# The output projection's seventh block product, split into quarter products

## The chip, the cores and the metric

The kernel runs on one core of one Trainium2 chip. The metric is the device time of one execution in microseconds (us). The core's engines are TensorE (matmuls; "PE" in the profile, with "PEld" for its weight loads), VectorE ("DVE"), ScalarE ("ACT"), GpSimd ("POOL") and SyncE ("SP"), which here issues all DMAs. Each engine takes its own instructions strictly in the order in which the program wrote them, and waits for other engines at semaphores.

## The reference

Two attention layers, one after the other, over eight images of 512 channels and 32 x 32 = 1024 positions, in float32. Cut to what matters, for one layer and with `w` and `b` as its weights:

```python
xn  = group_norm(x) * gn_scale + gn_bias          # 8 groups in layer 0, 32 in layer 1
qkv = einsum('oc,bcn->bon', qkv_w, xn) + qkv_b
q, k, v = split into 8 heads of 64 channels
att = softmax(einsum('bhdi,bhdj->bhij', q, k) / 8, axis=-1)
out = einsum('bhij,bhdj->bhdi', att, v)           # back to 512 channels
x   = einsum('oc,bcn->bon', proj_w, out) + proj_b + x
```

The change concerns the last line, the output projection with its residual `x`: a product of a 512 x 512 matrix with a 512 x 1024 matrix, a bias for each row, and the old `x` added.

## The kernel before, in words

The work is cut into sixteen units, one for each image of each layer. Pass u of the main loop (u from 0 to 15) runs the projections to q, k and v of unit u (`projections`), then the output projection of the unit before it, u − 1 (`project`), and then the attention of unit u (`attention`). So fifteen output projections run in this way, in passes 1 to 15; the last unit's runs after the loop (`project_last`). Below, "pass 5" means the pass of unit 5, with the output projection of unit 4 in it. Layer 0 is units 0 to 7, layer 1 units 8 to 15. The order on every engine is the order in which these Python functions are called; there is no scheduler (`manual_schedule`).

A product of two large matrices is not formed directly. `blocks` cuts both factors into 2 x 2 blocks and forms seven block products in place of eight (Winograd's variant of Strassen's method), with sums and differences of the blocks made beforehand on VectorE and GpSimd. The left factors are sums of weight blocks (`mix_weights`), the right ones sums of data blocks (`mix_right`, whose four parts are called `mixing`). The seven products are formed in the order 1, 6, 2, 7, 5, 4, 3. They accumulate in three pairs of PSUM banks, which `blocks` calls `bx`, `by` and `bz`; they are the same as `apair[0]` (called `x` in the plans), `sbank[0]` and `apair[1]` (called `z`). A fourth pair, `sbank[1]`, is called `s1`. Products 1 and 2 use `bx`, products 6, 7 and 4 accumulate one after the other in `by`, products 5 and 3 in `bz`. Between them VectorE takes sums out of `by`: after product 6 `u2 = by + p1`, after product 7 `u3 = by + p1`, where `p1` is the copy of product 1 that ScalarE made. A result block is named by its row half r and its column half h: (0, 0) comes after product 2, (1, 1) after product 5 as `bz + u3`, (1, 0) after product 4 as `by + p1`, (0, 1) after product 3 as `bz + u2`. `done` is called after each of the seven, with a count g.

A block product may itself be formed in quarters: `inner_products` cuts its 2 x 2 factor blocks once more and forms seven small products of 128 x 128 by 128 x 256 in place of four matmuls of 128 x 128 by 128 x 512. Four of these small products (1, 6, 7 and 5 of the inner order) don't go to the block's own bank: 1, 6 and 7 accumulate in a region `one`, 5 goes into a region `two`, and after each of the four ScalarE copies the region to an SBUF tile of the rest (`m2`, `m4` and so on, "m_o" in the profile). GpSimd then adds two quarters of the rest together (`fold`, L468 and L469) and adds the rest to every result block that the product belongs to (`rests`). An entry of `plan` gives the inner product's `one`, `two`, order and room. Which block products are formed in quarters stands in `INNER`; in the output projection ("o") it is products 2, 3 and 4.

An inner product wants its own left and right factors. The right ones ("ro" in the profile) are made in `mix_o` by four VectorE subtractions of 128 x 256, and the left ones ("lo") were made once for each layer by GpSimd or VectorE (`mix_inner_left`), stored in DRAM, and are loaded in each pass; in pass 9, the first to use those of layer 1, they are made on the spot by GpSimd (`make_left`). All of this is hung into the projections of the next unit by the dictionary `parts`: `parts[g]` runs after the g-th block product of the q, k and v projections, of which 15 to 21 belong to v.

What is particular to passes 7 and 9: in pass 7 GpSimd and VectorE also make the inner left factors of q and k for layer 1 (`made_parts`, ten parts of four operations), some in the projection at g = 3, the others on VectorE at fixed steps of the attention (`left_parts`), and VectorE mixes weights of layer 1. In pass 9 it is the output projection's turn.

In `project`, `done` adds the bias and `x` (the tiles `w.res`) to `u2`, `u3` and `p1` by pairs of L703; `others` adds PSUM to these sums (L737); `rests` adds a rest and stores the result (L745, `store`).

The attention of a unit has eight chunks of eight steps. In each step TensorE forms scores (L820), ScalarE their exponentials (L828), VectorE sums these (L865, L867) and TensorE multiplies by v (L848). Its first scores need the bank that `others(1, 0)` has just emptied, and its third those of `others(0, 1)`.

Of the kernel before, what the change touches and what calls it, by code (L numbers as in the profile page):

```python
# [18 lines left out]
P = 128  # L19
# [13 lines left out]
def fast_path(ctx, tc, x, qkv_wT, proj_wT, vecs, groups, out, flag):  # L33
# [24 lines left out]
    BL = 32  # L58
    SCALE = 1.0 / math.sqrt(D)

    INNER = {"q": (2, 5, 4, 3), "k": (1, 2, 7, 5, 4, 3), "o": (2, 3, 4)}
    assert D == H and C == FD

    def pool(name, bufs, **kw):
# [477 lines left out]
    def room_of(pool, tag):  # L542
        return lambda name: pool.tile([P, 2, FD], F32, tag=tag, name=name)
# [151 lines left out]
    def project(w, after):  # L695


        l, b = units[w.u]
        dst = mid[b] if l == 0 else out[b]
        g = 0  # L700

        def plus(to, o, cols, more):
            return nc.vector.scalar_tensor_tensor(  # L703
                to, cols, vec[:, l, PB, o : o + 1], more, ALU.add, ALU.add
            )

        def done(sums):

            nonlocal g
            g += 1  # L710
            for i in range(2):
                if g == 2:
                    u2 = sums[1][:, i, :]
                    plus(u2, i, w.res[i][:, FD:], u2)
                elif g == 4:
                    u3 = sums[2][:, i, :]
                    plus(u3, 2 + i, w.res[2 + i][:, FD:], u3)
                elif g == 5:
                    p1 = sums[0][:, i, :]
                    plus(p1, 2 + i, w.res[2 + i][:, :FD], p1)  # L720
            after(g)

        results = {}

        def store(o, h):
            nc.sync.dma_start(dst[o * P : (o + 1) * P, ts(h, FD)], results[o, h])

        def c11(bank, *_):
            for i in range(2):
                cols = results[i, 0] = w.res[i][:, :FD]  # L730
                plus(cols, i, bank[:, i, :], cols)

        def others(r, h, bank, more, _=None):
            for i in range(2):
                o = 2 * r + i
                results[o, h] = more[:, i, :]
                w.evac[h] = nc.vector.tensor_add(more[:, i, :], bank[:, i, :], more[:, i, :])  # L737
                if (r, h) == (1, 1):
                    store(o, h)

        def rests(r, h, rest, _):
            for i in range(2):
                o = 2 * r + i
                cols = results[o, h]
                nc.gpsimd.tensor_add(cols, cols, rest[:, i, :])  # L745
                store(o, h)

        w.evac = [None, None]
        x, z, s1 = apair[0], apair[1], sbank[1]
        tmp = room_of(tmppool, "tmp")  # L750
        plan = {
            2: (s1, z, ORDER, tmp), 4: (x, s1, ORDER, tmp), 3: (s1, x, ORDER, room_of(accpool, "acc"))
        }
        inner = {k: (*w.inner_o[k], *plan[k]) for k in w.inner_o}
        w.taken = blocks(
            f"o_{w.u}", w.left, w.right_o, False, c11, others, done, (rbpool, "rb"), plain_sum, inner, rests
        )

# [26 lines left out]
    def attention(w, at_step, at_end):  # L785
# [189 lines left out]
        def bias_last():  # L975
# [4 lines left out]

        parts = {
            3: [lambda: reciprocals(CC - 1)], 10: [lambda: divide(CC - 1)], 14: [bias_last],
            17: mixing[:2], 21: [mixing[3], mixing[2]],
        }

        w.inner_o = {}
# [14 lines left out]
        def make_left(i):  # L1001
            w.making[i](lefts[3 * i : 3 * i + 3], later=behind_loads)

        def mix_o(k):
            tag = {2: "x2", 3: "x1", 4: "x4"}[k]
            room = tpool.tile([P, 4, FD2], F32, tag=tag, name=f"ro{k}_{u}")
            if k == INNER["o"][-1]:
                w.inner_o[k] = mix_inner_in(w.right_o[k], room, nc.vector)
                lefts.append(room[:, 3, :P])
                if u == B:  # L1010
                    make_left(2)
                else:
                    nc.sync.dma_start(lefts[-1], src[:, len(lefts) - 1, :])
            else:
                w.inner_o[k], subs = mix_inner(w.right_o[k], room, nc.vector)
                for part in subs:
                    part()
# [3 lines left out]
                w.inner_o[k] = (inner_lefts(k, w.left[k], lefts[3 * i : 3 * i + 3]), w.inner_o[k])  # L1021

        parts[15] = [load_left]
        if u == B:
            parts[20] = [partial(make_left, 0), partial(make_left, 1)]
        parts[18] = [partial(mix_o, 2)]
        parts[21] += [partial(mix_o, 4), partial(mix_o, 3)]
        w.finish = finish
        return parts

# [36 lines left out]
    for u in range(2 * B):  # L1067
# [84 lines left out]
        if old is not None:  # L1152
# [4 lines left out]
            def after(g):  # L1157
                stats_of(*stats_after.get(g, ()))
                if u == B - 1:
                    for part, room in zip(made_parts[:3], rooms) if g == 3 else ():  # L1160
                        part(room)

            project(old, after)
            if u == B - 1:
                left_v, mixing_w = mix_weights(1, load_weights(1, (2,)), nc.vector, 2)
                lefts = lefts + left_v
                left_parts = {
                    (c, 3 if c else 6): partial(made_later, c, part)
                    for c, part in enumerate(made_parts[3:])
                }  # L1170
            w.evac_before, w.taken_before = old.evac, old.taken
            if u == B:
# [313 lines left out]
```

## Time and profile before

| what | us |
|---|---|
| median of 8 runs | 3258.44 |
| lowest and highest of the runs | 3258.10, 3259.56 |
| the profiled execution, by its own time | 3258.73 |
| its span, first to last instruction | 3256.9 |
| granted TensorE clock | 1.000 of full speed |
| an attention (pass 5, 893.15 to 1003.41) | 110.26 |
| projections to q, k and v (pass 5, 801.83 to 870.26) | 68.43 |
| the output projection (pass 5, 870.26 to 893.15) | 22.89 |

The time of an execution is the span and some 1.8 us around it. A row of the timeline has a start, a length, the engine, the line of the code, the operation, the tile that is written and those that are read, and the number of like instructions merged into it; in brackets is the time for which the engine stood idle before it, and who ended that. Tile names leave buffer numbers out: `s` is one of the two `sbank`s, `a` one of the `apair`s. Busy times of the engines in three projections and in the first chunk of an attention, from the view by stretches:

```profile
core 0: us, PE busy (x) PEld busy (x) DVE busy (x) ACT busy (x) POOL busy (x), PEclk, DMA share, GB/s
870.26:893.15 22.89, 22.89 (x76) 13.85 (x74) 20.77 (x32) 5.12 (x12) 7.07 (x8) 1.00 0.53 205
1475.02:1497.91 22.89, 22.89 (x76) 13.85 (x74) 22.21 (x33) 5.11 (x12) 13.21 (x20) 1.00 0.64 240
1879.98:1902.87 22.89, 22.89 (x75) 13.85 (x73) 22.49 (x32) 5.11 (x12) 14.61 (x18) 1.00 0.61 209
893.15:906.90 13.75, 13.75 (x129) 5.00 (x132) 11.82 (x11) 8.36 (x9) 5.66 (x5) 1.00 0.21 79
```

The first row is pass 5, an ordinary one; the second is pass 7 and the third pass 9.

### The profile page before, as it was taken

To read this page: it belongs to the slowest core of one execution; us is meant where nothing else is said; L and a number is where in the kernel's file an instruction comes from. 1 tells how busy PE (TensorE), PEld (TensorE's weight loads), DVE (VectorE), ACT (ScalarE), POOL (GpSimd) and SP (SyncE) were. 2 spreads that over 40 slices of the span, in tenths; PEclk is the share of its full clock that TensorE was granted. 3 is DMA by queue.
4 is the path that set the end of the run, shared out by engine and by line. 5 is a ranking of instruction groups with operands and counts; after the bars stand their busy time and mean duration, and the time that the engine had idled before them with its cause. 6 is when DMAs were issued, how large, how long until landed. Compare 5 with 4: busy or idle time off the path is not lost.

```text
span 3256.9 us, 56805 instructions
## 1 busy us (share of the span) xinstructions
PE 3244.3 (100%) x22206; PEld 1863.4 (57%) x22206; DVE 2714.5 (83%) x3488; ACT 1650.8 (51%) x2296; POOL 1215.3 (37%) x1207
## 2 busy tenths in 40 slices
PE   9999999999999999999999999999999999999999
PEld 5465474654746547465574655747556474564743
DVE  5887978789787897989979889797897978979786
ACT  1653627546274463744637446373563735537354
POOL 2054171531706317063270732607126071350710
PEclk9999999999999999999999999999999999999999
DMA  3112120121201212023120121201212012120111
GB/s 104 48 45 79 46 79 28 45 79 46 85 22 45 85 44 85 18 71 114 55 86 27 45 86 46 86 15 45 86 46 85 17 49 81 46 85 22 68 70 48
DMA packets 86464, 192.51 MB, mean 59 GB/s; under 512 B 22961, under 2 KB 34993, under 8 KB 84273
## 3 DMA queue, kind: packets, MB, share of 16 engines
q1 hardware_dynamic: 86192, 188.82, 16.9%
q8 instruction: 180, 2.95, 0.4%
q14 instruction: 92, 0.75, 0.1%
HBM read 148.00 MB, written 39.19 MB: 57 GB/s over the span
## 4 chain that ended last, share of the span: by engine, by line
PE 96%; DVE 3%; issue 0%; DMA 0%; ACT 0%; SPq 0%; DVEq 0%
PE a L848 26%; PE s L820 25%; PE s L416 14%; PE a L416 12%; PE a L455 10%; PE s L455 9%; DVE acc L867 1%; PE a L820 1%; PE s L766 0%; PE a L766 0%; DVE tr L880 0%; PE s L361 0%; DVE acc L865 0%; DVE ao L874 0%; DMA xn<-x_dram 0%
## 5 line engine op out<-in xcount | busy, mean ns | idle before, releaser
L828 ACT ACTIVATE p<-s 128x1024 f32<-128x1024 f32 x976 | 998.5, 1025 | 557.8 <-PE s L820 514.9
L848 PE MATMUL a<-p,v 64*64 64x512 f32 x8192 | 1099.9, 589 | 0.0
L820 PE MATMUL s<-q,k 64*64 64x512 f32 x7808 | 1058.2, 590 | 0.0
L867 DVE TENSOR_TENSOR acc<-acc,p 128x1024 f32<-128x1024 f32 x768 | 967.9, 1260 | 61.5 <-ACT p L828 12.8
L848 PEld LDWEIGHTS a<-p,v 64*64 64x64 f32 x8192 | 383.3, 131 | 495.8 <-ACT p L828 350.3
L820 PEld LDWEIGHTS s<-q,k 64*64 64x64 f32 x7808 | 383.6, 133 | 431.8 <-issue 422.6
L1088 POOL TENSOR_TENSOR r<-xn 128x256 f32<-128x256 f32 x30 | 49.5, 1649 | 1175.8 <-DVE acc L867 1038.3
L650 POOL TENSOR_TENSOR k<-k,m_k 128x512 f32<-128x512 f32 x180 | 259.5, 1462 | 0.0
L865 DVE TENSOR_TENSOR acc<-p,p 128x1024 f32<-128x1024 f32 x128 | 156.6, 1224 | 21.7 <-ACT p L828 13.9
L312 POOL TENSOR_TENSOR y<-var,half 128x4 f32<-128x4 f32 (+1 forms) x17 | 33.2, 1951 | 344.2 <-DVE var L310 344.2
L880 DVE STREAM_TRANSPOSE tr<-acc 128x1024 f32<-128x1024 f32 x128 | 158.0, 1234 | 0.0
L650 POOL TENSOR_TENSOR q<-q,m_q 128x512 f32<-128x512 f32 x120 | 157.2, 1325 | 0.0
L890 DVE TENSOR_REDUCE red<-tr 128x32 f32<-128x1024 f32 x128 | 154.4, 1207 | 0.6
L538 DVE TENSOR_TENSOR u_v<-s,p_v 128x1024 f32<-128x1024 f32 x32 | 39.2, 1224 | 123.8 <-PE s L416 123.8
L501 ACT COPY p_o<-a 128x1024 f32<-128x1024 f32 x15 | 15.2, 1013 | 244.2 <-PE a L416 244.2
L874 DVE TENSOR_TENSOR ao<-a,tmp 128x512 f32<-128x512 f32 x128 | 88.1, 688 | 60.9 <-ACT tmp L873 59.8
L460 ACT COPY m_q<-s 128x256 f32<-128x256 f32 x150 | 55.9, 373 | 145.3 <-PE s L455 142.8
L468 POOL TENSOR_TENSOR m_o<-m_o 128x256 f32<-128x256 f32 x45 | 34.3, 762 | 251.5 <-ACT m_o L460 251.5
L416 PE MATMUL s<-x_t,s2w 128*128 128x512 f32 x256 | 117.5, 592 | 0.0
L416 PE MATMUL a<-w,xn 128*128 128x256 f32 x496 | 112.1, 379 | 0.0
L460 ACT COPY m_k<-s 128x256 f32<-128x256 f32 x165 | 61.5, 373 | 93.7 <-PE s L455 90.2
L334 ACT ACTIVATE xn<-xn,shift,scale 128x512 f32<-128x512 f32 x124 | 99.6, 805 | 10.8 <-DVE shift L330 10.8
(291 smaller groups left out, 5129.1 us busy)
## 6 DMA issues: line engine op xcount, KB each, us to landing
rb<-drec SPq DMA_DIRECT2D x128, 256.0 KB, 3.9
xn<-mid SPq DMA_DIRECT2D x36, 512.0 KB, 7.6
il<-ilk SPq DMA_DIRECT2D x15, 1152.0 KB, 6.7
xn<-x_dram SPq DMA_DIRECT2D x32, 512.0 KB, 7.2
x<-x_dram SPq DMA_DIRECT2D x32, 512.0 KB, 5.4
x<-mid SPq DMA_DIRECT2D x28, 512.0 KB, 4.7
il<-ilq SPq DMA_DIRECT2D x15, 768.0 KB, 4.2
mid<-u_o SPq DMA_DIRECT2D x32, 256.0 KB, 2.0
```

Source lines behind the costliest of these rows:

```text
L334: nc.scalar.activation(cols, cols, AF.Identity, bias=st["shift"][:, c - lo : c - lo + 1], scale=st["scale"][:, c - lo : c - lo + 1],)
L416: nc.tensor.matmul(dst, at[:, c, ts(i, P)], moving[:, c, :], start=start and c == 0 and not (tokens and i % 2), stop=stop and c == 1, skip ...
L455: nc.tensor.matmul(dst[j], a[j], b[j], start=j in (1, 5) or first and j in (2, 4), stop=j not in (1, 6), skip_group_check=True,)
L460: taken.append(nc.scalar.copy(to[j], dst[j]))
L650: w.last[sel].append(add(cols, cols, rest[:, i, :]))
L820: nc.tensor.matmul(bank[e * H : (e + 1) * H, j, :], w.k[pr][j * H : (j + 1) * H, t * P + e * H : t * P + (e + 1) * H], w.q[pr][j * H : (j ...
L828: exp = nc.scalar.activation(p, bank, AF.Exp, scale=SCALE)
L848: nc.tensor.matmul(banks[r][j * H : (j + 1) * H, :], w.v[rows, t, lo : lo + D], p[rows, j, :], start=(t == 0), stop=(t == NT - 1),)
L865: nc.vector.tensor_add(acc, state["first"], p)
L867: nc.vector.tensor_add(acc, acc, p)
L880: nc.vector.transpose(tr, state["acc"].pop(c))
L890: nc.vector.tensor_reduce(red[:, :, qh, :], state["tr"].rearrange("p j (f i) -> p j f i", i=BL), AX.X, ALU.add)
```

## The change

The seventh block product of the output projection is formed in quarters too. For that it gets right factors (`mix_o(7)`, in a tile of `accpool`, made one block product earlier than those of 4 and 3, together with the difference that it needs, `mixing[3]`), left factors (two of them in that tile, two in the tile of product 4), regions (`s1` and `z`; product 2 now takes `z` and `s1` in place of `s1` and `z`) and a room for its rest (tile "o2"; the rest of product 3 moves from `accpool` to "o1"). Its rest is added to two result blocks: (1, 1), which is now stored after that addition and not straight after `others`, and (1, 0), which is stored after the second of its two additions. The bias and `x` are added to `p1` at g = 4 and no longer at g = 5. In passes 0 and 9 there are four parts of left factors to be made and not three. In pass 7 two parts of those of q and k, not three, are made by GpSimd in the projection, and VectorE makes one more in the attention, at step 6 of its second chunk.

```diff
-    INNER = {"q": (2, 5, 4, 3), "k": (1, 2, 7, 5, 4, 3), "o": (2, 3, 4)}
+    INNER = {"q": (2, 5, 4, 3), "k": (1, 2, 7, 5, 4, 3), "o": (2, 3, 7, 4)}
...
-                elif g == 5:
+            for i in range(2):
+                if g == 4:
                     p1 = sums[0][:, i, :]
                     plus(p1, 2 + i, w.res[2 + i][:, :FD], p1)
...
-                if (r, h) == (1, 1):
-                    store(o, h)
-
-        def rests(r, h, rest, _):
+
+
+        to_come = [(1, 0)]
+
+        def rests(r, h, rest, _=None):
             for i in range(2):
                 o = 2 * r + i
                 cols = results[o, h]
                 nc.gpsimd.tensor_add(cols, cols, rest[:, i, :])
-                store(o, h)
+                if (r, h) not in to_come:
+                    store(o, h)
+            if (r, h) in to_come:
+                to_come.remove((r, h))
...
-            2: (s1, z, ORDER, tmp), 4: (x, s1, ORDER, tmp), 3: (s1, x, ORDER, room_of(accpool, "acc"))
+            2: (z, s1, ORDER, tmp), 7: (s1, z, ORDER, room_of(tpool, "o2")),
+            4: (x, s1, ORDER, tmp), 3: (s1, x, ORDER, room_of(tpool, "o1")),
...
-            17: mixing[:2], 21: [mixing[3], mixing[2]],
+            17: mixing[:2], 20: [mixing[3]], 21: [mixing[2]],
...
-            tag = {2: "x2", 3: "x1", 4: "x4"}[k]
-            room = tpool.tile([P, 4, FD2], F32, tag=tag, name=f"ro{k}_{u}")
-            if k == INNER["o"][-1]:
+            pool, tag = {2: (tpool, "x2"), 7: (accpool, "acc"), 3: (tpool, "x1"), 4: (tpool, "x4")}[k]
+            room = pool.tile([P, 4, FD2], F32, tag=tag, name=f"ro{k}_{u}")
+            if k in (7, 4):
                 w.inner_o[k] = mix_inner_in(w.right_o[k], room, nc.vector)
-                lefts.append(room[:, 3, :P])
-                if u == B:
-                    make_left(2)
-                else:
-                    nc.sync.dma_start(lefts[-1], src[:, len(lefts) - 1, :])
+                n = len(lefts)
+                lefts.extend(room[:, 3, i * P : (i + 1) * P] for i in range(2))
+                if u != B:
+                    nc.sync.dma_start(
+                        room[:, 3, :].rearrange("p (s o) -> p s o", s=2), src[:, n : n + 2, :]
+                    )
...
         parts[15] = [load_left]
+        parts[18] = [partial(mix_o, 2)]
+        parts[20].append(partial(mix_o, 7))
+        parts[21] += [partial(mix_o, 4), partial(mix_o, 3)]
         if u == B:
-            parts[20] = [partial(make_left, 0), partial(make_left, 1)]
-        parts[18] = [partial(mix_o, 2)]
-        parts[21] += [partial(mix_o, 4), partial(mix_o, 3)]
+            parts[20] += [partial(make_left, i) for i in range(3)]
+            parts[21].append(partial(make_left, 3))
...
-                    for part, room in zip(made_parts[:3], rooms) if g == 3 else ():
+                    for part, room in zip(made_parts[:2], rooms) if g == 3 else ():
...
+                when = [(0, 6), (1, 3), (1, 6)] + [(c, 3) for c in range(2, 7)]
                 left_parts = {
-                    (c, 3 if c else 6): partial(made_later, c, part)
-                    for c, part in enumerate(made_parts[3:])
+                    at: partial(made_later, i, part)
+                    for i, (at, part) in enumerate(zip(when, made_parts[2:]))
                 }
```

## The prediction

> **What bounds the kernel now.** I read the page first, then the waits of TensorE, then instruction times of one projection pass, and last the two passes that carry extra work.
>
> ```profile
> PE 3244.3 (100%) x22206; PEld 1863.4 (57%) x22206; DVE 2714.5 (83%) x3488; ACT 1650.8 (51%) x2296; POOL 1215.3 (37%) x1207
> ...
> PE 96%; DVE 3%; issue 0%; DMA 0%; ACT 0%; SPq 0%; DVEq 0%
> ```
>
> TensorE is busy from end to end, and the chain of waits is TensorE for 96%. The list of what TensorE waited for has four entries, 5.8 us in all, none in a projection:
>
> ```profile
> PE s L361 <- DMA xn<-x_dram: 4.4, 1, 4.4
> PE s L416 <- DVE xn L179: 0.6, 1, 0.6
> PE a L292 <- DVE e L305: 0.6, 1, 0.6
> ```
>
> So a row less on TensorE is time less, unless a wait takes its place. The timeline of TensorE in the projection run in the pass of unit 5 (start, length, instruction) gives the prices. One fp32 matmul is two rows.
>
> ```profile
> 877.12 0.59 PE L455 MATMUL s<-ao,wproj_wproj 128*128 128x256 f32 x2
> ...
> 880.14 3.60 PE L416 MATMUL s<-ao,wproj_wproj 128*128 128x512 f32 x8
> 883.58 3.60 PE L416 MATMUL a<-o_t,s1w 128*128 128x512 f32 x8
> 887.01 0.59 PE L455 MATMUL a<-o_t,wproj_wproj 128*128 128x256 f32 x2
> ...
> 890.03 0.59 PE L455 MATMUL s<-ao,s4w 128*128 128x256 f32 x2
> 890.47 0.59 PE L455 MATMUL a<-ao,s4w 128*128 128x256 f32 x2
> ```
>
> Lengths overlap, so only starts count. Product 2 in quarter products takes 880.14 − 877.12 = 3.02 us (seven steps of 0.431); products 7 and 5, whole, take 3.43 each. The whole projection, first product at 870.26 to first score at 893.15, is 22.89; its parts are 4 x 3.43 + 3 x 3.02 = 22.8 and 0.1 at the end. All fifteen last 22.9. They have no stall to win back.
>
> VectorE in the same pass:
>
> ```profile
> 870.46 1.23 DVE L675 TENSOR_TENSOR v<-a,u_v 128x1024 f32<-128x1024 f32 x1 [2.23 <-PE a L416]
> ...
> 877.42 1.23 DVE L538 TENSOR_TENSOR u_o<-s,p_o 128x1024 f32<-128x1024 f32 x1 [0.42 <-PE s L416]
> ...
> 883.78 1.23 DVE L538 TENSOR_TENSOR u_o<-s,p_o 128x1024 f32<-128x1024 f32 x1 [0.57 <-PE s L416]
> 885.04 1.42 DVE L703 SCALAR_TENSOR_TENSOR u_o<-x,vec,u_o 128x512 f32<-128x512 f32 x2
> ...
> 887.27 1.29 DVE L737 TENSOR_TENSOR u_o<-a,u_o 128x512 f32<-128x512 f32 x2 [0.21 <-issue]
> 888.48 1.41 DVE L703 SCALAR_TENSOR_TENSOR p_o<-x,vec,p_o 128x512 f32<-128x512 f32 x2
> ```
>
> In brackets is idle time before. There are 2.23 us of it just where new work goes; later there is little. Two passes are fuller: in that of unit 9 (new weights of layer 1 are made on GpSimd) the first of these sums starts 8.22 us after the projection's start, not 7.16, and in unit 7's it follows other work without a gap at 7.31:
>
> ```profile
> 1888.20 1.22 DVE L538 TENSOR_TENSOR u_o<-s,p_o 128x1024 f32<-128x1024 f32 x1
> ```
>
> **What the Trainium skill says.** "Perfetto Trace Analysis", section Identifying the Most-Contended Engine: busy matmuls are a bad measure of the distance to the roof, since they are pipelined. The trace agrees: rows last 0.59 us and start 0.43 per pair; hence starts. "SBUF — State Buffer", section SBUF: two separate sides: VectorE with two SBUF inputs and GpSimd share a port pair as an exclusive lock. The trace agrees in kind: a 128x128 GpSimd operation of 0.46 us takes 1.44 beside VectorE's subtractions in pass 9, which grow from 0.42 to 0.67 there, and a pair of L703 from 1.41 to 1.89.
>
> **The change, part by part.**
>
> *TensorE.* Per projection four 512-column matmuls (3.43 us) become seven of 256 (3.02): −0.41, fifteen times: −6.2 us. Nothing else on TensorE changes in number.
>
> *The four copies of the new partial regions* (ACT, 0.37 each) find ACT idle: it works 5.12 of 22.89 us there. A region is written again only after its copy. Product 7's last such region, z, is finished at step five of seven; its copy starts 0.2 later, ends 2.7 after the product's start, and product 5 writes z at 3.02. Products 4 and 3 have this distance today (s1 after x, s1), without a stall. Product 2's swap to (z, s1) needs z free at 6.9 after the start; VectorE empties it by 1.7, in pass 7 by about 4.8. Cost 0; without this cover it would be some 0.3 a pass.
>
> *Right sides.* Four subtractions of 128x256 (about 0.34 apart, 0.42 long: 1.5 to 1.75 us in sum) and one of 128x1024 (1.14) move to the gap of 2.23 before the last sum of the values. That sum, at 870.46, slips to some 870.9 (868.2 + 1.14 + 1.5), and what follows is shorter by the moved 1.14: the mixing ends no later. Cost 0 in the thirteen ordinary passes. In pass 7 no gap is there: +1.5 us on VectorE.
>
> *x added sooner.* The pair of L703 on p_o (1.33 from start to next start) goes ahead of the pair L737 that frees z. Product 3's second step writes z. Ordinary pass, from the projection's start: bn_stats ends 12.95; the sum L538 to 14.2; two pairs L703 to 16.85; bn_stats to 17.5; L737 to 18.7. Product 3 starts at 3 x 3.43 + 3 x 3.02 = 19.36, its second step at 19.8. Slack 1.1; GpSimd's new fold (2 x 0.73) then holds the shared port, which I price with 0.5 from the 1.41 to 1.89 above: 0.6 left. No wait. Behind that step stand all of product 3 and the next attention.
>
> Pass 7: first sum at 8.8, not 7.3; L737 ends near 20.3 and TensorE wants z at 19.8: a wait of 0.5 to 1.0, I take 0.7. Pass 9: first sum at 8.2 to 8.6 with VectorE slowed throughout, L737 ends at 20.2 to 21.1: a wait of 0.4 to 1.3, I take 1.1 as four more GpSimd operations prolong the contention. Together 1.8.
>
> *GpSimd.* A fold, two additions on (1,1), two on (1,0): 1.45 + 2.5 + 2.5 = 6.5 us a pass. Its last addition in pass 5, over at 898.9, moves to about 902.9, 10 us into attention, where GpSimd has nothing until a power in the second chunk. Three of its readers: p_o's store is 3 us later, but its buffer is next used in chunk 1, since the first accumulator now takes that of the new right side; u_o's store leaves behind an addition; tile o1 is wanted by VectorE in pass 7 at step 6, some 2 us later than free. Cost 0, up to 0.5 in pass 7 if it isn't free.
>
> *SP.* One DMA more per pass (1 KB a row, 0.33 us of queue) ahead of the loads of x, with the buffer long free: 0. In pass 0 four more GpSimd operations, three DMAs and a wait for a reused tile delay the queue; the load of the next input goes from 87.4 to about 89.5; its first part lands some 4 us after issue, at 93.5, and is needed at 95.2: 0. Pass 7's weight part moves from GpSimd to VectorE at step 14 (four rows, 0.9 us) where VectorE idles 0.37 + 0.96: 0, at most 0.5.
>
> **Sum.** −6.2 + 1.8 = −4.4. The profiled execution took 3258.73 (span 3256.9 and 1.8 around it): 3254.3. The runs' median, 3258.44, is 0.3 lower: 3254.0.
>
> **Rivals.**
> 1. *No waits at all*, also in passes 7 and 9: 3258.44 − 6.2 = 3252.2. For it: product 4 has slack at 9, and a reader waits only for the last of two halves. Against: pass 9's VectorE has no gap left.
> 2. *The port contention reaches every pass.* If VectorE is 0.8 later than I work out, past the 0.6 that is left, z comes 0.2 late in thirteen passes: +2.6, 3256.6. For it: the stretched rows in 7 and 9. Against: L737 reads PSUM, so has one SBUF input.
> 3. *Slower.* The same place: L737 behind the moved L703. Beyond 0.41 us of waiting a pass the product's gain is gone; it decides once VectorE is 0.6 + 0.41 = 1.0 later than I work out. At 0.9 of waiting in all fifteen: 3258.4 + 7.3 = 3266. Against: VectorE loses 1.1 us from the projection itself.
> 4. *More than the arithmetic*: the 0.9 us stalls around unit 7's norm (L305) and the next unit's mixing (L179) shift away: 3251.
>
> **Numbers.** Main case 0.55, rival 1 0.16, rival 2 0.20, rival 3 0.05, rival 4 0.04. The range 3252.0 to 3256.8 takes in rivals 1 and 2 and the bounds of the two waits. About 0.2%, 6.5 us, can be told from no change: the whole arithmetic gain lies just under it. Faster by over that: rival 4 and the edge of 1, 0.07; slower 0.05; within 0.88.
>
> **What would show it.** Projections of 22.5 us in ordinary passes, the seventh at 3.02; passes 7 and 9 longer by 0.5 to 1.3, with the gap before product 3's second step and L737 of VectorE named; the first sum at 7.2 after the start elsewhere; GpSimd's last addition 4 us later. Wrong if ordinary passes show a gap there, or before product 5 (copies), or if the first attention or unit 8's start grows.

## The result, and the profile after

The changed kernel took 3268.38 us (median of 12 runs, 3267.58 to 3269.94) against 3258.42 for the kernel before beside it (32 runs): a ratio of 1.0031, with a 95% interval of 1.0023 to 1.0038. It is 10 us slower; 4.4 us less had been predicted. The interval is about 2.4 us to either side, so 10 us stand clear of it (the prediction had put what can be told at 6.5 us). The profiled span went from 3256.9 to 3266.1.

Where the 9.2 us of span lie follows from the starts of TensorE's first products and first scores in each pass:

| stage | before | after | sum of the differences |
|---|---|---|---|
| thirteen output projections | 22.89 each | 22.48 each | −5.3 |
| those of passes 7 and 9 | 22.89, 22.89 | 24.46, 24.44 | +3.1 |
| attentions of passes 1, 3 to 6, 8, 10 to 14 | 110.26 each | 110.87 to 110.89 | +6.8 |
| attentions of passes 2 and 9 | 110.26 each | 111.25 each | +2.0 |
| attention of pass 7 | 111.09 | 113.96 | +2.9 |
| attentions of passes 0 and 15 | 110.40, 110.03 | 110.40, 110.03 | 0 |
| all else (start, projections to q, k and v, end) | | | −0.3 |

So the gain in the projections came as worked out (0.41 each), and most of the loss, 11.7 us, is in the attentions, to whose own code the change adds only one weight part in pass 7. The two long projections cost 3.1. Of the attentions, only those lose that have an output projection before them and a next unit's norm inside.

The page of the changed kernel: VectorE has 76 us more of busy time, and its share of the chain of waits went from 3% to 5%. GpSimd has 161 us more, where the prediction's 6.5 us a projection make 98 in fifteen.

```profile
PE 3241.8 (99%) x22296; PEld 1923.5 (59%) x22296; DVE 2790.5 (85%) x3552; ACT 1673.8 (51%) x2356; POOL 1376.5 (42%) x1301
...
PE 93%; DVE 5%; issue 1%; POOL 1%; ACT 0%; DMA 0%; SPq 0%; DVEq 0%; POOLq 0%; ACTq 0%
```

The list of TensorE's waits in the changed kernel (us in total, times, longest) names two new places; what the dots leave out is the wait for the first input (4.7), which the kernel before has too (4.4). In the changed kernel's numbering L738 is the former L737, L747 the former L745, L871 and L873 the sums of exponentials (formerly L865 and L867), L826 the scores; L292 and L305 are as before.

```profile
PE a L292 <- DVE e L305: 6.7, 14, 1.4
...
PE a L455 <- DVE u_o L738: 3.1, 2, 1.7
PE a L292 <- DVE mv L284: 1.8, 1, 1.8
```

L292 is a tiny product in the middle of the attention: the next unit's group norm sends its statistics through TensorE to sum them over the rows of a group, first the means (`mv`, attention step 11), then, at step 13, a vector `e` that VectorE makes of the means. All scores behind this product in TensorE's order wait for `e`. The wait of 1.8 on the means is in pass 7 alone.

VectorE's timeline in pass 5, first the kernel before, whose attention starts at 893.15:

```profile
896.34 1.42 DVE L865 TENSOR_TENSOR acc<-p,p 128x1024 f32<-128x1024 f32 x1 [1.03 <-ACT p L828]
897.86 7.43 DVE L867 TENSOR_TENSOR acc<-acc,p 128x1024 f32<-128x1024 f32 x5
905.66 1.23 DVE L867 TENSOR_TENSOR acc<-acc,p 128x1024 f32<-128x1024 f32 x1 [0.37 <-ACT p L828]
908.71 0.69 DVE L874 TENSOR_TENSOR ao<-a,tmp 128x512 f32<-128x512 f32 x1 [1.82 <-ACT tmp L873]
...
916.04 0.16 DVE L305 TENSOR_TENSOR e<-d,mv 128x4 f32<-128x4 f32 x1
```

and then the changed kernel, whose attention starts at 893.80:

```profile
896.93 1.93 DVE L871 TENSOR_TENSOR acc<-p,p 128x1024 f32<-128x1024 f32 x1 [0.97 <-ACT p L834]
898.96 11.21 DVE L873 TENSOR_TENSOR acc<-acc,p 128x1024 f32<-128x1024 f32 x6
910.09 0.68 DVE L880 TENSOR_TENSOR ao<-a,tmp 128x512 f32<-128x512 f32 x1
...
917.41 0.16 DVE L305 TENSOR_TENSOR e<-d,mv 128x4 f32<-128x4 f32 x1
```

Six sums took 7.43 + 1.23 = 8.66 and take 11.21; the first took 1.42 and takes 1.93. These 3.1 us in all eat the idle time of 0.37 + 1.82 in the first chunk, and `e` starts 23.61 after the attention's start, not 22.89. GpSimd at that time, its last additions in the kernel before and then the changed kernel:

```profile
895.40 3.49 POOL L745 TENSOR_TENSOR u_o<-u_o,m_o 128x512 f32<-128x512 f32 x2
```

```profile
894.02 5.97 POOL L747 TENSOR_TENSOR p_o<-p_o,m_o 128x512 f32<-128x512 f32 x4
899.95 1.71 POOL L468 TENSOR_TENSOR m_o<-m_o 128x256 f32<-128x256 f32 x1
901.74 1.60 POOL L469 TENSOR_TENSOR m_o<-m_o 128x256 f32<-128x256 f32 x1
903.29 4.47 POOL L747 TENSOR_TENSOR u_o<-u_o,m_o 128x512 f32<-128x512 f32 x2
```

It works until 907.76, 14.0 us into the attention; in the kernel before it was done at 898.9. Its own rows are stretched too: a fold of 0.73 takes 1.6 to 1.7. TensorE shows the price, with the idle time in brackets (here 0.39 of the 0.6 that the attention grew by; the rest lies in rows around it):

```profile
917.72 0.22 PE L292 MATMUL a<-e,gmat 64*64 64x4 f32 x2 [0.39 <-DVE e L305]
```

The other place is the second step of product 3 in passes 7 and 9, which the prediction had named. TensorE's row there in pass 7, 0.43 after the last one if nothing held it:

```profile
1495.99 0.59 PE L455 MATMUL s<-ao,s4w 128*128 128x256 f32 x2
1498.30 0.70 PE L455 MATMUL a<-ao,s4w 128*128 128x256 f32 x2 [1.72 <-DVE u_o L738]
```

### The profile page after: what moved, and what is told of

Read it like the earlier page. It is cut to its first block, busy times and chain, and to the rows that moved or that the text cites. A ratio compares the mean times of both kernels' runs of the same rounds, so it can differ in the third digit from the quotient of the medians.

```text
span 3266.1 us, 57313 instructions
## 1 busy us (share of the span) xinstructions
PE 3241.8 (99%) x22296; PEld 1923.5 (59%) x22296; DVE 2790.5 (85%) x3552; ACT 1673.8 (51%) x2356; POOL 1376.5 (42%) x1301
## 4 chain that ended last, share of the span: by engine, by line
PE 93%; DVE 5%; issue 1%; POOL 1%; ACT 0%; DMA 0%; SPq 0%; DVEq 0%; POOLq 0%; ACTq 0%
PE a L854 24%; PE s L826 24%; PE s L416 12%; PE a L416 12%; PE a L455 10%; PE s L455 9%; DVE acc L873 2%; PE a L826 1%; DVE acc L871 1%; DVE tr L886 1%; DVE red L896 0%; PE s L772 0%; PE a L772 0%; ACT p L834 0%; POOL u_o L747 0%
## 5 line engine op out<-in xcount | busy, mean ns | idle before, releaser
L854 PE MATMUL a<-p,v 64*64 64x512 f32 x8192 | 1115.0, 589 | 0.0
L826 PE MATMUL s<-q,k 64*64 64x512 f32 x7808 | 1073.2, 590 | 0.0
L873 DVE TENSOR_TENSOR acc<-acc,p 128x1024 f32<-128x1024 f32 x768 | 1005.9, 1310 | 57.3 <-ACT p L834 6.7
L854 PEld LDWEIGHTS a<-p,v 64*64 64x64 f32 x8192 | 400.0, 131 | 479.2 <-ACT p L834 337.0
L826 PEld LDWEIGHTS s<-q,k 64*64 64x64 f32 x7808 | 413.4, 133 | 402.3 <-issue 394.1
L871 DVE TENSOR_TENSOR acc<-p,p 128x1024 f32<-128x1024 f32 x128 | 163.0, 1273 | 17.6 <-ACT p L834 16.5
L468 POOL TENSOR_TENSOR m_o<-m_o 128x256 f32<-128x256 f32 x60 | 58.7, 978 | 167.1 <-ACT m_o L460 167.1
L747 POOL TENSOR_TENSOR u_o<-u_o,m_o 128x512 f32<-128x512 f32 x60 | 104.6, 1764 | 44.1 <-DVE u_o L738 44.1
L460 ACT COPY m_o<-a 128x256 f32<-128x256 f32 x120 | 44.7, 373 | 138.1 <-PE a L455 136.3
```

The lines of the kernel that those rows point to most:

```text
L460: taken.append(nc.scalar.copy(to[j], dst[j]))
L826: nc.tensor.matmul(bank[e * H : (e + 1) * H, j, :], w.k[pr][j * H : (j + 1) * H, t * P + e * H : t * P + (e + 1) * H], w.q[pr][j * H : (j ...
L854: nc.tensor.matmul(banks[r][j * H : (j + 1) * H, :], w.v[rows, t, lo : lo + D], p[rows, j, :], start=(t == 0), stop=(t == NT - 1),)
L871: nc.vector.tensor_add(acc, state["first"], p)
L873: nc.vector.tensor_add(acc, acc, p)
```

## The experiments

Theory A: the added GpSimd additions lie beside VectorE's sums in the first chunk and the two hinder each other in reading SBUF (the shared port pair of the prediction); VectorE falls behind, `e` comes late, TensorE stands before L292. Rival B: some buffer or store that waits for the longer GpSimd holds up the attention. Rival C: x added sooner puts VectorE behind for the whole pass. The results in one table; the ratio is to runs of the kernel before on the same chip (medians from 3258.13 to 3258.44), the stages are from the profiles in us (projection in ordinary passes and in 7 and 9, attention likewise). A profile is one execution, and the time to its first scores alone lies between 86.3 and 88.3 us in these seventeen, so that the stages of a row and its median agree to some 2 us and no better. e3 has 4 runs, e8 7, all others 12 or more.

| run | median us | ratio, 95% interval | proj. | 7 | 9 | att. | 7 | 9 |
|---|---|---|---|---|---|---|---|---|
| kernel before | 3258.42 | | 22.89 | 22.89 | 22.89 | 110.26 | 111.09 | 110.26 |
| changed kernel | 3268.38 | 1.0031 [1.0023, 1.0038] | 22.48 | 24.46 | 24.44 | 110.88 | 113.96 | 111.25 |
| e1, norm one step later | 3259.03 | 1.0003 [0.9994, 1.0012] | 22.48 | 24.46 | 24.44 | 110.26 | 113.17 | 110.59 |
| e2, no second rest | 3256.32 | 0.9995 [0.9986, 1.0004] | 22.48 | 24.45 | 24.50 | 110.26 | 111.84 | 110.26 |
| e3, before + additions | 3284.21 | 1.0080 [1.0063, 1.0097] | 22.89 | 22.89 | 22.89 | 111.86 | 115.33 | 111.97 |
| e4, before + memsets | 3258.36 | 1.0001 [0.9992, 1.0009] | 22.89 | 22.89 | 22.89 | 110.26 | 111.09 | 110.26 |
| e7, before + copies | 3260.66 | 1.0008 [1.0000, 1.0017] | 22.89 | 22.89 | 22.89 | 110.26 | 113.15 | 110.26 |
| e5, x later | 3265.38 | 1.0023 [1.0014, 1.0031] | 22.48 | 23.70 | 24.57 | 110.71 | 114.79 | 110.81 |
| e6, x and norm later | 3264.95 | 1.0021 [1.0012, 1.0029] | 22.48 | 23.70 | 24.60 | 110.71 | 115.31 | 110.81 |
| e8, other tile | 3268.03 | 1.0030 [1.0018, 1.0042] | 22.48 | 24.46 | 24.11 | 110.88 | 113.76 | 111.24 |
| e9, statistics in attention | 3262.37 | 1.0013 [1.0006, 1.0020] | 22.48 | 22.49 | 23.16 | 110.26 | 116.48 | 112.55 |
| e10, before, as e9 | 3263.71 | 1.0016 [1.0009, 1.0023] | 22.89 | 22.89 | 22.89 | 110.26 | 114.56 | 111.41 |
| e11, the same, norm in chunk 4 | 3261.71 | 1.0010 [1.0004, 1.0017] | 22.48 | 22.51 | 23.34 | 110.26 | 117.47 | 112.27 |
| e12, before, as e11 | 3264.32 | 1.0018 [1.0011, 1.0026] | 22.89 | 22.89 | 22.89 | 110.26 | 114.96 | 111.07 |
| e13, e1 + weight part back | 3260.44 | 1.0007 [0.9998, 1.0015] | 22.48 | 24.45 | 24.33 | 110.26 | 116.89 | 110.57 |
| e14, e1 + norm late in 7, 9 | 3260.19 | 1.0004 [0.9996, 1.0013] | 22.48 | 24.45 | 24.46 | 110.26 | 114.70 | 110.26 |
| e15, e14 + some statistics later | 3259.56 | 1.0003 [0.9995, 1.0011] | 22.48 | 23.14 | 23.80 | 110.26 | 114.48 | 110.26 |

**e1.** The changed kernel, with only this:

```diff
-        "stats": (), "norm": (9, 11, 13, 16),
+        "stats": (), "norm": (9, 11, 14, 17),
```

> The changed kernel with the third and fourth part of the next unit's norm (TensorE's small matmul L292 on e, and the scaling) one attention step later: 9, 11, 14, 17. Theory A (GpSimd's longer run slows VectorE's sums in the first chunk, e of L305 comes 0.7 us late, and TensorE stands before that one matmul): a step is 1.7 us, more than the lateness, so 14 attentions lose their 0.62 us each; 3268.4 - 8.7 = 3259.7, the projections stay at 22.48 and the two long ones at 24.4. Rival B (a buffer or a store that waits for GpSimd delays the attention): nothing in it asks for e, 3268 stays. Rival C (x added sooner puts VectorE behind for the whole pass): the wait moves to the next reader, 3266 to 3268.

3259.03: 9.35 us come back, where A said 8.7, and the ordinary attentions stand at 110.26 (one at 110.35). VectorE is as late as in the changed kernel (`e` starts 23.60 after the attention's start); only TensorE no longer asks so soon. That settles where the time went, and B falls as an explanation of the loss in ordinary passes: no store or buffer was moved. It doesn't say why VectorE is late. C has VectorE behind from the projection on, but its first sum starts 3.13 after the attention's start in the changed kernel and 3.19 in the kernel before: it falls behind within the first chunk. The next three runs ask by what.

**e2.** The changed kernel without the seventh rest on block (1, 0), a part of the sum that is left out here:

```diff
-        if seventh is not None:
+        if seventh is not None and name[0] != "o":
             rests(1, 0, seventh)
...
-        to_come = [(1, 0)]
+        to_come = []
```

> The changed kernel without the two GpSimd additions of the seventh rest to block (1, 0) (that part of the sum is left out), with its store after the one addition that is left. Theory A: 2.5 us of GpSimd's work alone, some 3.5 to 4.5 us under contention, are taken out of the first chunk of each attention; VectorE's lateness of 0.72 at e shrinks below 0.4 and the attention's extra 0.62 to 0 to 0.3: 3260 to 3264. Rival B: GpSimd is also sooner with the stores, so the same fall, no distinction. Rival C: unchanged, 3268.

3256.32, below the expected 3260 to 3264: two of GpSimd's additions fewer, and the attentions are at 110.26 again. GpSimd is done 9.5 us into the attention, not 14.0; VectorE's six sums take 9.99, which its idle time can still take, and `e` starts at 22.90:

```profile
897.67 9.99 DVE L873 TENSOR_TENSOR acc<-acc,p 128x1024 f32<-128x1024 f32 x6
```

The first chunk's 2.2 us of idle time act as a threshold. With the first sum counted, a stretch of 1.3 us (e2) costs an ordinary attention nothing, 3.1 (changed kernel) cost 0.6, and 4.0 (e3, below) cost 1.6. Pass 7's attention falls from 113.96 to 111.84: 2.1 of its 2.9 us go with these two additions.

**e3, e4 and e7.** The kernel before, with work on GpSimd behind each projection's last addition that nobody waits for, on an unread tile:

```diff
+        spare = tpool.tile([P, 2, FD], F32, tag="o2", name=f"spare_{w.u}")
+        for i in range(4):                                   # e3
+            nc.gpsimd.tensor_add(spare[:, i % 2, :], q[i][:, :FD], q[i][:, FD:])
+        for i in range(2):
+            nc.gpsimd.tensor_add(spare[:, i, :FD2], q[i][:, :FD2], q[i][:, FD2:FD])
...
+        for i in range(10):                                  # e4
+            nc.gpsimd.memset(spare[:, i % 2, :], 0.0)
...
+        for i in range(8):                                   # e7
+            nc.gpsimd.tensor_copy(spare[:, i % 2, :], q[i % 4][:, :FD])
```

> The kernel before, with six more GpSimd additions behind each output projection's last one (four of 128x512 and two of 128x256, from tiles of q to a tile that nobody reads): as much GpSimd work as the change adds, and nothing else of the change; no store or buffer waits for it. Theory A: VectorE's sums in the first chunk stretch from 1.2 to 1.4 up to 1.9, e comes late, and 14 attentions grow by 0.4 to 0.8 us: 3264 to 3269, projections at 22.89. Rivals B and C: nobody waits for these additions and VectorE has its old order, 3258.4 +- 0.6.

> The kernel before, with ten GpSimd memsets of 128x512 on the same unread tile in place of those six additions: GpSimd is busy for several us more in the same place but reads no SBUF operand. Theory A in its narrow form (additions with two SBUF operands on both engines hinder each other): VectorE's sums keep their 1.2 to 1.4 us and the time stays at 3258.4 +- 0.6. If any GpSimd work in that place delays the attention (GpSimd's queue, its later power, or writes alone): 3262 to 3268.

> The kernel before with eight GpSimd copies of 128x512 from tiles of q to the unread tile, behind the last addition of each output projection: GpSimd reads one SBUF operand, not two. If only GpSimd operations with two SBUF operands hold up VectorE's sums, these stay at 1.2 to 1.4 us and the time at 3258.4 +- 0.6. If any SBUF read of GpSimd does, the sums stretch as with the dummy additions and the time is 3264 to 3284.

The additions cost more than expected (3284.21): the attentions grow by 1.6 (unit 3's by 3.8), because here the product on the means (step 11) waits as well. VectorE and GpSimd in pass 5 of e3:

```profile
905.94 12.65 DVE L873 TENSOR_TENSOR acc<-acc,p 128x1024 f32<-128x1024 f32 x6
```

```profile
906.93 8.90 POOL L761 TENSOR_TENSOR spare<-q 128x512 f32<-128x512 f32 x4
915.80 3.38 POOL L763 TENSOR_TENSOR spare<-q 128x256 f32<-128x256 f32 x2
```

Single rows of both, taken in narrower windows of that timeline:

```profile
910.38 2.11 DVE L873 TENSOR_TENSOR acc<-acc,p 128x1024 f32<-128x1024 f32 x1
...
909.15 4.47 POOL L761 TENSOR_TENSOR spare<-q 128x512 f32<-128x512 f32 x2
```

A sum beside such additions takes 2.11, where one alone takes 1.23, and an addition 2.2, where one alone takes 1.25. TensorE's list of waits has 13.9 us on the means (14 times) and 5.3 on `e`. The memsets, in the same place in e4, leave VectorE's rows at the lengths of the kernel before (the sums of exponentials are L870 in e4 and e7):

```profile
898.54 7.43 DVE L870 TENSOR_TENSOR acc<-acc,p 128x1024 f32<-128x1024 f32 x5
906.35 1.23 DVE L870 TENSOR_TENSOR acc<-acc,p 128x1024 f32<-128x1024 f32 x1 [0.38 <-ACT p L831]
```

```profile
899.51 4.71 POOL L760 MEMSET spare<- 128x512 f32 x10
```

So the loss can be made without the change, and it goes with GpSimd's reading of SBUF, not with its being busy or writing. (The memsets end 10.4 us into the attention, the additions of e3 later; but e2's additions, over at 9.5, did stretch the sums.) One SBUF operand is enough: in e7 the six sums take 9.86, between the two. The first stands beside the last of the old additions, and each of the other five, beside copies, takes 1.45:

```profile
903.44 1.45 DVE L870 TENSOR_TENSOR acc<-acc,p 128x1024 f32<-128x1024 f32 x1
```

In ordinary passes the idle time covers that; pass 7, which is full, loses 2.06.

**e5 and e6.** The changed kernel with x and the bias added to p1 at g = 5 again, e6 also with the norm at 9, 13, 15, 18:

```diff
-            for i in range(2):
-                if g == 4:
+                elif g == 5:
                     p1 = sums[0][:, i, :]
                     plus(p1, 2 + i, w.res[2 + i][:, :FD], p1)
```

> The changed kernel with x and the bias added to p1 at g = 5 again, as in the kernel before; all else of the change stays. If the waits of 1.96 us before product 3's second step in passes 7 and 9 come from the pair of L703 on p_o that now stands ahead of L738 (1.4 us alone, up to 1.9 beside GpSimd), these two fall to 0 to 0.6 each, and the ordinary projections stay at 22.48; if they come from the new subtractions ahead of the first sum alone, they stay near 1.96. Theory A has GpSimd's work unchanged, so the attentions keep their 0.6 extra: 3268.4 - 3.2 = 3265.2. Rival C (x added sooner puts VectorE behind in every pass) has the attentions back at 110.26: 3256.

> The changed kernel with both: x and the bias on p1 at g = 5 again, and the norm of the next unit at steps 9, 13, 15, 18. Theory A: attentions at 110.26, also those of passes 2 and 9, where 0.99 was lost; pass 7, where two stalls before L292 come to 3.9 us (2.25 on the means, 1.86 on e), keeps at most about 1 of its extra 2.9; projections at 22.48, those of 7 and 9 at most 0.6 longer. Sum: 3258.3 - 15 x 0.41 + 0 to 2 = 3252.2 to 3254.2, below both kernels. If the delay has another seat than that matmul and L738, it stays above 3257.

e5's total was as expected (3265.38), but not for the reason given: pass 9's projection didn't shorten, and the 0.45 us that ordinary attentions still lose have moved. e6's total missed (3264.95, where 3252.2 to 3254.2 had been expected). In these two kernels the lines stand one lower than in the changed kernel: L737 is its L738, L746 its L747, L825 the scores. The waits of TensorE in e6; e5's list has the same row:

```profile
PE a L825 <- DVE u_o L737: 3.1, 14, 0.3
```

Now the attention's first steps wait for the banks that L737 empties. The reason is in VectorE's and GpSimd's timelines of e5, pass 5:

```profile
888.02 3.05 DVE L703 SCALAR_TENSOR_TENSOR p_o<-x,vec,p_o 128x512 f32<-128x512 f32 x2
890.99 1.27 DVE L737 TENSOR_TENSOR p_o<-s,p_o 128x512 f32<-128x512 f32 x2
```

```profile
887.58 2.94 POOL L746 TENSOR_TENSOR u_o<-u_o,m_o 128x512 f32<-128x512 f32 x2 [1.82 <-DVE u_o L737]
890.48 1.18 POOL L468 TENSOR_TENSOR m_o<-m_o 128x256 f32<-128x256 f32 x1
```

At g = 5 the pair of L703, which reads x and p_o, stands beside the new additions and takes 3.05 in place of 1.40; L737, which has a PSUM operand, keeps 1.27. With the pair at g = 5, VectorE is late at the attention's start, and the wait there stands in the place of the one for `e`: e5 is 3.0 us faster than the changed kernel, but e6 is 5.9 slower than e1, which differs in the pair's place and in norm steps that are as late or later. So once the norm asks later, the pair is better at g = 4. Rival C is not borne out: adding x later didn't bring VectorE forward in ordinary passes. Why pass 9's projection didn't shorten stays open.

**e8.** Pass 7's left parts in other tiles; the first of them had VectorE standing for GpSimd's last addition to release the tile:

```diff
-            room = left_rooms(f"l{i}_{u}", tpool, ("o1", "o2", "o4")[i % 3], 2 * FD)[0]
+            room = left_rooms(f"l{i}_{u}", tpool, ("o4", "o2", "o1")[i % 3], 2 * FD)[0]
```

> The changed kernel with the tiles of pass 7's left parts in the order o4, o2, o1 in place of o1, o2, o4. In the changed kernel product 3's rest lies in o1, so the first part (attention step 6) makes VectorE stand 1.17 us until GpSimd's last addition has read that tile. If that wait is a cause of its own in pass 7: that attention falls from 113.96 to 112.3 to 113.1, all others keep their extra 0.6, 3267.0 to 3267.6. If only the shared port matters there, it stays at 113.7 to 114.1, 3268.4.

113.76, and the total stayed: what had been expected if only the port matters there. The same row of VectorE's timeline, in the changed kernel and then in e8:

```profile
1517.33 0.29 DVE L226 TENSOR_TENSOR l<-w 128x128 f32<-128x128 f32 x1 [1.17 <-POOL u_o L747]
```

```profile
1517.42 1.36 DVE L226 TENSOR_TENSOR l<-w 128x128 f32<-128x128 f32 x1
```

The semaphore wait is gone and the subtraction takes 1.36 in place of 0.29: GpSimd's addition is still running beside it and ends at 1518.63, the subtraction 0.15 later. Rival B is real in this one place, but removing it gave back 0.2, since the wait came back inside the row.

**e9 to e12.** The changed kernel with the norm of e1 and, in passes 7 and 9, all eight bn_stats (L280, the statistics of the next unit's norm) moved from the projection into the attention, at steps 9 to 19 (e9) or 10 to 22 (e11), with the norm behind them; pass 7's left parts later. e10 and e12 are the kernel before with the same moves. The core of e9:

```diff
+    MID = {
+        "stats": (9, 11, 12, 13, 14, 15, 18, 19), "norm": (20, 22, 27, 30),
+        "apply": (32, 33, 36, 38, 39, 41, 43, 44),
+    }
...
+            if u in (B - 1, B + 1):
+                stats_after = {}
...
-            plan = LATE if u == 0 else USUAL
+            plan = LATE if u == 0 else MID if u in (B - 1, B + 1) else USUAL
```

> The changed kernel with: the norm at 9, 11, 14, 17; in passes 7 and 9 all eight bn_stats out of the projection and into attention steps 9 to 19, with the norm behind at 20, 22, 27, 30; pass 7's left parts from step 15 on. Theory A and the reading that passes 7 and 9 wait because VectorE is 2 us behind ahead of L738: four bn_stats, 2.5 us, leave the queue ahead of L738, so both projections come to 22.5 to 22.7; attentions 2 to 6 and 8 to 14 at 110.26, that of 7 at 110.3 to 111. Sum: 3258.3 - 6.2 + 0.2 to 1.2 = 3252.3 to 3253.3. If the waits in 7 and 9 have another cause, they stay and it gives 3255 to 3257.

> The kernel before with the same moves of norm, bn_stats and left parts, without the seventh product in quarters. It had a stall of 0.83 us in pass 7's attention and no other there, so 3257.4 to 3258.4; what the run above is below this is the product alone, 15 x 0.41 = 6.2 us if nothing is given back.

> The changed kernel with the norm at 9, 11, 14, 17; in passes 7 and 9 the bn_stats in attention steps 10 to 22, the norm behind at 23, 28, 30, 33, so that TensorE's two small matmuls come five steps after the statistics are asked for and not two; pass 7's left parts from chunk 2, step 6, to chunk 6, step 4. The stalls of 3.5 and 1.8 us that the earlier placing met before L292 in passes 7 and 9, and 1.6 at unit 8's start, should be gone: attentions of 7 and 9 at 110.3 to 110.8, projections at 22.48, that of pass 9 at 23.2. Sum: 3258.3 - 6.2 + 0.7 + 0 to 1 = 3252.8 to 3253.8. If VectorE in pass 7 can't catch up by step 28, 3255 to 3257.

> The kernel before with the same moves and without the seventh product in quarters: its one stall of 0.83 in pass 7 may go, so 3257.4 to 3258.4. The run above should lie 5.0 to 5.6 below it: 15 x 0.41 less the 0.7 left in pass 9's projection.

The projections did as expected: 22.49 and 22.51 in pass 7, 23.16 and 23.34 in pass 9. The two waits before product 3 are VectorE's lateness ahead of L738. All four totals missed: in these two placings VectorE didn't take 5 us of statistics in pass 7's attention without new waits, on the norm again (first row, e9, where the VectorE row named stands just behind the making of the means) or also, in e11 (the two others), on exponentials whose tiles are still to be summed:

```profile
PE a L292 <- DVE one L913: 4.5, 2, 3.1
```

```profile
PE a L854 <- ACT p L834: 3.6, 4, 1.4
PE a L292 <- DVE e L305: 3.3, 2, 1.7
```

The kernel before loses with these plans too (3.5 and 3.9 in that attention). Each plan with the product in quarters is faster than the same plan without it, by 1.3 (e9 against e10) and 2.6 us (e11 against e12). That is the split's worth beside an equal plan; 6.2 and 5.0 to 5.6 had been expected, and most of the rest is lost in longer attentions of passes 7 and 9.

**e13 to e15.** e1's kernel, with pass 7's third weight part made by GpSimd in the projection again (e13); with the norm of passes 7 and 9 at 23, 28, 30, 33 (e14); and that with their bn_stats one each at g = 3, 4 and 6 and five at g = 7 (e15):

```diff
-                    for part, room in zip(made_parts[:2], rooms) if g == 3 else ():
+                    for part, room in zip(made_parts[:3], rooms) if g == 3 else ():
...
+    MID = {
+        "stats": (), "norm": (23, 28, 30, 33),
+        "apply": (36, 38, 39, 41, 43, 44, 46, 47),
+    }
...
+            if u in (B - 1, B + 1):
+                stats_after = {3: (0,), 4: (1,), 6: (2,), 7: (3, 4, 5, 6, 7)}
```

> Against the run with the norm one step later (3259.0, pass 7's attention 113.17, its projection 24.46): the third weight part is made by GpSimd in the projection again and not by VectorE at chunk 1, step 6. If that part is the cause, pass 7's attention falls to 111 to 112; as GpSimd then works 1.7 us longer beside VectorE, its projection may grow from 24.46 to 24.5 to 25.5. If it is not the cause, the attention stays at 112.8 to 113.5 and the time at 3259 to 3260.

> Against the same run: in passes 7 and 9 alone the norm at 23, 28, 30, 33, with its applications from 36; statistics and weight parts stay where the change has them. If TensorE loses time in that attention only at the two small matmuls, in front of a late VectorE, pass 7 comes from 113.17 to 110.3 to 110.8 and pass 9 from 110.59 to 110.26: 3259.0 - 2.9 = 3255.8 to 3256.2. If VectorE is too late for other readers as well (exponentials that wait for tiles it has not yet summed), pass 7 stays above 111.5.

> The run just above with, in passes 7 and 9, one bn_stats each at g = 3, 4 and 6 and five at g = 7, in place of three, one, two and two: two of them, 1.2 us, leave the queue ahead of L738 of block (1, 1), and three, 1.8 us, that ahead of L738 of block (0, 1); the first chunk gets 1.9 us more. If the waits are VectorE's lateness there, these projections come from 24.45 to 22.6 to 23.3 and the total to 3252.8 to 3254.4; if the first chunk can't take the work, the attentions of 7 and 9 grow by up to 2 and it stays at 3256.

e13: pass 7's attention grows to 116.89. GpSimd starts its last additions later, and VectorE, which wants tile o1 for the next left part, stands:

```profile
1515.63 0.29 DVE L226 TENSOR_TENSOR l<-s4w 128x128 f32<-128x128 f32 x1 [3.09 <-POOL u_o L747]
```

So taking the part back makes pass 7 worse; what the part alone costs VectorE isn't shown, since GpSimd's additions moved with it. e14: pass 9 is at 110.26, but pass 7 got worse (114.70): the wait of 1.8 on the means at step 11 is gone, and one of 2.3 on `e` at step 30 has come. VectorE has not caught up by then. The rest of the growth was not traced. e15 halves the waits in the projections (23.14, 23.80) and the attentions don't grow further, but pass 7's stays at 114.48.

No version that forms the whole sum beat the kernel before: e1, e13, e14 and e15 can't be told from it.

## Why the prediction was wrong

Step by step, as it stands above:

The prediction's sum was −6.2 + 1.8 = −4.4. The span shows, in the same terms, −6.15 for TensorE, +3.94 for the two waits, +11.7 for the attentions, which had stood at 0, and −0.3 elsewhere: +9.2.

- *TensorE, −0.41 a projection*: right, 22.48 in thirteen passes.
- *Copies, SP, pass 0's queue at 0*: right; no wait names them, and pass 0's attention kept 110.40.
- *Right sides at 0 in ordinary passes*: right. The first of VectorE's sums starts 7.17 after the projection's start (7.2 was given), in pass 7 at 8.79 (8.8).
- *x added sooner, slack of 0.6 left*: right. L738 of block (1, 1) ends 19.28 after the start, where 18.7 and 0.5 for the port had been worked out, and no ordinary pass waits there.
- *The waits in passes 7 and 9, 0.7 and 1.1*: the right place, too small; they measured 1.98 and 1.96 (24.46 and 24.44 less 22.48). L738 ended 21.6 after the start in both, against 20.3 and 20.2 to 21.1. In pass 7 the missing 1.3 are three pairs of L703 beside GpSimd, at 2.04, 1.75 and 1.80 in place of 1.41; the sum took them at their lengths alone, though two of these pairs had taken 1.82 and 1.79 in pass 7 of the kernel before. In pass 9 the first sum started at 9.31, not by 8.6, and two pairs took 1.98 and 1.68.
- *GpSimd, cost 0*: **this step failed.** It said that the last addition moves "to about 902.9, 10 us into attention, where GpSimd has nothing until a power in the second chunk", and went through buffers and readers. It asked what GpSimd would be late for, not whom it would hinder. The prediction had found the shared port pair, but applied it to the projection alone. Its reading of pass 9 was also off: the GpSimd operation of 1.44 stands not beside the subtractions that grow from 0.42 to 0.67 (there it takes 0.63), but beside 128x1024 differences (L179, 1.45 and 1.47 in place of 1.22). Read so, it says that one operation waits out most of the other, whatever its own length. In the attention VectorE's sums read two SBUF operands each, so they and the additions slow each other: the additions ended 14.0 us into the attention, not 10, and the sums lost 3.1 us where 2.2 of idle time stood. The profile of before showed all three terms: GpSimd's additions at the attention's start, to which 6.5 us were to come, a first chunk with 2.2 idle, and a first sum of 1.42 beside GpSimd's last additions (1.19 in the second chunk). Cost: 11.7 us over the attentions; the total fell by 9.4 when e1 moved one small product and the scaling behind it.
- *Pass 7's weight part, at most 0.5*: not measured by itself; taking it back cost more (e13). Of pass 7's 2.9 us, 2.1 go with the two additions on (1, 0) (e2), so most of it is the same contention, in a pass whose first chunk is fuller.

The third rival gave 3266, near the result by luck: it put the wait at the pair that frees z (now L738) in every pass, and no ordinary pass waits there. None of the named signs of being wrong came: no gap there or before product 5 in ordinary passes, the first attention at 110.40, unit 8's start at 69.25 (69.38 before). That the ordinary attentions could grow stood nowhere.

The Trainium skill's page "SBUF — State Buffer", section SBUF: two separate sides, says whom the lock concerns: besides VectorE's two-port modes, a VectorE operation with two SBUF inputs, and this only against a GpSimd operation that reads SBUF. The runs agree with both halves of the latter: additions stretched the sums (2.11 for 1.23), memsets did not (1.23). It was known; it was not carried to the stage into which the work moved.

What stays open: why passes 2 and 9 lose 0.4 us more in the attention than the ordinary ones (`e` comes 0.35 later there), and whether a plan exists that keeps passes 7 and 9 free of waits. Splitting pass 7's weight parts over other passes wasn't tried.

## What to carry to other kernels

When work on an engine off the critical path grows, place it in time and ask what it runs beside, not only who waits for it: here GpSimd and VectorE paid each other's time, and the idle time of the hindered one was all the cover there was. Small in-order products that depend on a nearly full engine (here the norm's) turn lateness that would be caught up later into time lost; ask for them later than they can first be had. A gain of 0.4 us in each of many passes can be lost in the two passes that are already full (with the ordinary attentions mended, in e1, the total is that of the kernel before), so price those by themselves, with stretched lengths.

## What the runs showed of the hardware

- The two engines take turns. With a queue of such work on both, VectorE's 128x1024 sums and GpSimd's 128x512 additions go in step, one of each every 2.2 us (lengths 2.11 and 2.25 in e3 with the wait in them; 1.23 and 1.25 alone). Each engine's rows look slow, and no wait is listed: the wait lies inside the row's length.
- What a pair of such operations takes is about 0.3 us less than both lengths alone: 2.2 for 1.23 + 1.25 (additions, e3), 1.67 for 1.23 + 0.73 (folds, changed kernel), 1.55 for 1.23 + 0.61 (128x512 copies, e7). So a copy with its one SBUF operand stretches a sum by less (to 1.45) in step with its being shorter; no sign of the number of operands shows in these three.
- A single short operation pays the rest of the other's: 1.36 for a subtraction of 0.29 (e8).
- Ten memsets of 128x512, which read nothing, took 4.71 and stretched nothing (e4).
